# Sixteen gathered blocks instead of fourteen in a graph layer with residual and normalisation

## Chip, cores and metric

The kernel runs on one core of a Trainium2 chip. The metric is device time in microseconds (us). Before the change, three runs gave a median of 632.7 us (629.24 to 637.61). One more execution, taken with the hardware profiler, is the source of every duration below; it took 545.63 us.

## The reference

A graph has 6250 nodes with 128 features each and 100,000 edges, sorted by their destination. An edge has a source, a destination and a type (0 or 1). Each edge carries the message of its source node, made with one of two weight matrices by the edge's type; messages are summed at the destination. The node's own row goes through a third matrix, and the result is added to the input and normalised.

```python
Xs = X[src]
m_data = Xs @ W_data.T + b_data
m_ctrl = Xs @ W_control.T + b_control
msg = jnp.where((edge_types == 0)[:, None], m_data, m_ctrl)
agg = jax.ops.segment_sum(msg, dst, num_segments=X.shape[0])
out = jax.nn.relu(agg + (X @ W_self.T + b_self))
x = _layernorm(x + out)
```

## The kernel before

**Blocks.** The 6250 nodes are 49 blocks of 128 rows (`NB`). Since edges are sorted by destination, the edges of one destination block lie in one window of 18 x 128 edges (`KT` = 18). The engines are named as in the profile: PE does matmuls, ACT and DVE work on tiles and empty PE's output, POOL issues indirect DMAs, SP issues plain ones.

**Build (up to about 90 us).** For every source node and both edge types, PE computes the message row (`y`, L460 and L462). The row is kept as three bf16 parts whose sum is the fp32 value, so it has 3 x 128 = 384 columns (`D3`); `take` and `leave` (L467 to 480) split it off. All message rows stay on the chip in `m3`, as 98 source tiles (49 blocks times two types, `NT`), and are also stored to a table in memory (`store`, L482).

**Packed destination blocks.** The first 35 blocks (`NPB`, the sum of `GROUPS`) are packed, in seven groups of five.

- Ranking (`ranks`, L550): for each of 18 columns of edges, matmuls with `tri` and `rest` (32-column strips of 128 rows, output `acc`, 490 columns for five blocks: 98 tiles times 5) count how many edges of the same source tile came before; DVE reads the count with a reduction (`slot`, L563). Each step needs the one before it. 
- Packing (`fill_a`, `fill_b`, `fill_c`, L569 to 705): edges get places in 32 slots per source tile; the lists are written to memory (`packed`) and read back spread over all partitions (`spread`, L712). Edges over 32 in a slot are listed, and their rows are gathered by an indirect DMA into `mixed` (L693 to 697), one per group, on POOL's queue.
- Per block, 25 rounds (`NS`): `gather` (L745) selects rows of `m3` with up to four matmuls of 384 columns into a PSUM tile `g_ps`, 98 in all; `evict` (L757) copies that tile to SBUF, on ACT, and for blocks of the last group on ACT or DVE; `add_up` (L771) adds it into the destination rows with four more matmuls (100 in all), through a one-hot matrix `hot_d` that DVE makes.

**Gathered destination blocks.** The other 14 blocks (`NG`) take their messages from the table: for each of their 18 columns, POOL issues one indirect DMA of 128 rows of 384 values (`gather_rows`, L854) into one of `MB` = 5 message tiles; DVE makes a one-hot matrix for six columns at once (`hot_g`, L866), and PE adds the tile with four matmuls (`gathered_sums`). A gather waits until the tile `MB` gathers earlier has been read by PE.

**Ends.** Each block gets its own row by 8 matmuls (`own_of`), is summed, and waits for normalisation by group: packed ones by `PIECES` (the last group in two pieces), gathered ones by `GQ` blocks (5, 5 and 4).

**Order.** All these loops are streams of steps with assumed costs. A planner (`Order`) runs once when the program is written: at each engine it takes, among the steps that can start, the one with the earliest due time, and the instructions are issued in that order. An engine then runs its list strictly in order. `due` (L388) sets the due times: packed blocks every `BLOCK` = 13.1 us from `BUILT` = 76 us on, gathers every `PACE` = 1.75 us; the groups' packing ends `AHEAD` = 26 us before the group is begun.

```python
free = [("gm", *gathered[i - MB])] if i >= MB else [*stored, "idx"]
yield step(("msg", j, k), {"G": PACE}, *free, lag=3.0 - PACE)
```

`PACE` is thus the planned distance of gathers and their assumed time on POOL.

Of the kernel before, what the change touches and what calls it, by code (L numbers as in the profile page):

```python
# [32 lines left out]
ES = ER // RJ  # L33
EPS = 1e-05

GROUPS = (5,)*7
Q = max(GROUPS)
NPG = len(GROUPS)
NPB = sum(GROUPS)
NG = NB - NPB  # L40
STARTS = [sum(GROUPS[:i]) for i in range(NPG)]
R = 32
# [58 lines left out]
def step(name, costs, *needs, lag=0.0):  # L101
    return as_tuple(name), costs, [as_tuple(n) for n in needs], lag
# [7 lines left out]
def kernel(  # L110
# [95 lines left out]
    with ExitStack() as main:  # L206
        sums_over_windows(main, tc, x, xt, edges, w, bias, table, packed, total,
                          add_parts, finish, load_rows, norm)
# [6 lines left out]
def sums_over_windows(ctx, tc, x, xt, edges, w, bias, table, packed, total,  # L215
# [67 lines left out]
    for j in range(RJ):  # L283
# [17 lines left out]
    counted = {n: const.tile([P, P, n], BF16, name=f"count{n}")  # L301
               for n in sorted({DC, CH, *GROUPS})}
    tri = const.tile([P, P], BF16, name="tri")
# [5 lines left out]
    slot_values = [const.tile([P, (Q + 1) // 2, NT], BF16, name=f"vs{i}") for i in range(2)]  # L309
    slot_b = {n: const.tile([P, R, n], BF16, name=f"slot{n}") for n in sorted({*GROUPS})}  # L310

# [70 lines left out]

    LEAD, BUILT = 8.0, 76
    BLOCK = 13.1
    PACE = 1.75
    AHEAD, FIRST = 26.0, 20

    def due(kind, *i):  # L388
        if kind in ("p", "g") and i[0] in ("root", "rooted", "scale", "apply", "out"):
            n = i[1] + 1  # L390
            return BUILT + 10 + (BLOCK * sum(p[2] for p in PIECES[:n]) if kind == "p" else PACE * KT * GQ * n)
        if kind in ("counted", "turned", "first"):
# [21 lines left out]
        if kind in ("win", "xs", "agg", "o", "whole", "sum"):  # L414
            b = i[0]
            begun = BUILT + (BLOCK * b if b < NPB else PACE * KT * (b - NPB))
            if kind == "win":
                return due("fields", blocks[b][0]) - 8 if b < NPB else BUILT - 20
            if b >= NPB:
                return begun + {"whole": PACE * KT + 2, "sum": PACE * KT + 5}.get(kind, 0)  # L420
            return begun + {"whole": BLOCK + 0.5, "sum": BLOCK + 3}.get(kind, 0.3 * BLOCK)
# [4 lines left out]
        if kind in ("gh", "gm", "msg"):  # L426
            k = i[1] * CH if kind == "gh" else i[1]
            return BUILT + PACE * (i[0] * KT + k) + {"msg": 0, "gh": 2, "gm": 5}[kind]
        n = GROUPS[i[0]]
# [402 lines left out]
    rel_g = const.tile([P, NG, KT], BF16, name="rel_g")  # L832
    msgs, g_hots, kept = {}, {}, []
    GQ = -(-NG // -(-NG // Q))
    MB, XB = 5, 2

    def gathered_fields():
        yield step("idx", {"V": 1.8}, ("y", NB * 3 // 4), *[("win", b) for b in range(NPB, NB)])
# [10 lines left out]
    def gather_rows():  # L849
        for i, (j, k) in enumerate(gathered):  # L850
            free = [("gm", *gathered[i - MB])] if i >= MB else [*stored, "idx"]
            yield step(("msg", j, k), {"G": PACE}, *free, lag=3.0 - PACE)
            msgs[j, k] = late.tile([P, D3], BF16, name="msg", bufs=MB)
# [190 lines left out]
```

## Time and profile before

| what | value |
|---|---|
| median of three runs | 632.7 us |
| the profiled execution | 545.63 us |
| its span, first to last instruction | 543.9 us |
| mean granted clock of PE | 0.989 of full speed |
| PE busy | 504.0 us, 93% |
| DVE, ACT, POOL busy | 425.9, 422.6, 296.4 us |
| gathers | 252, first at 88.7 us, last at 520.4 us |
| DMA traffic | 79.20 MB, 146 GB/s in the mean |

A group's row gives the line, engine, operation, what it writes and reads, the count, then busy time and the mean duration of one in ns, then idle time of the engine before these instructions and what ended it. Durations of matmuls overlap, four strips of 32 columns run side by side, and so their sum is far above the busy time. L232 is a helper, `by_columns`, that issues four matmuls; the tiles tell which loop it served.

### The profile page before, as it was taken

What the parts mean: (1) busy time and instruction counts of PE and PEld (TensorE: products, weight loads), DVE (VectorE), ACT (ScalarE), POOL (GpSimd) and SP (SyncE); (2) the same over time, 40 slices, a digit from 0 to 9 for tenths busy, and PEclk for the clock granted to TensorE, in tenths of its full rate; (3) what the DMA queues carried; (4) which work ended last, traced back from release to release, by engine and by line L of the source; (5) the groups of instructions that cost most, each with busy time, mean ns of one, the idle gap of its engine ahead of it and who ended that gap; (6) DMA issues with size and microseconds to landing.
All of it is one profiled execution on the core that took longest, in us unless ns stands there. A gap on an engine that the chain in (4) does not pass through costs nothing.

```text
span 543.9 us, 26402 instructions
## 1 busy us (share of the span) xinstructions
PE 504.0 (93%) x11222; PEld 440.7 (81%) x11222; DVE 425.9 (78%) x958; ACT 422.6 (78%) x1012; POOL 296.4 (54%) x267
## 2 busy tenths in 40 slices
PE   4899978999899999999999999999999999979990
PEld 3555538799789999898998989989988898869990
DVE  4677679778887889888799788988798766867872
ACT  6745556697778888879879797798789987978782
POOL 1000004776766667767487576676677556676610
PEclk9999989999999999999999999999999999999996
DMA  3466984444454443645445445444355542646211
GB/s 110 134 178 189 285 278 136 147 142 124 138 149 154 140 128 128 174 124 156 139 137 153 134 140 169 155 147 118 114 179 169 160 140 62 194 143 189 91 46 30
DMA packets 60934, 79.20 MB, mean 146 GB/s; under 512 B 15761, under 2 KB 51372, under 8 KB 60808
## 3 DMA queue, kind: packets, MB, share of 16 engines
q1 hardware_dynamic: 47253, 48.95, 28.0%
q0 software_dynamic: 12400, 25.08, 16.9%
q10 hardware_dynamic: 1154, 3.41, 1.8%
q8 instruction: 89, 1.46, 1.1%
q14 instruction: 38, 0.30, 0.2%
HBM read 64.35 MB, written 13.05 MB: 142 GB/s over the span
## 4 chain that ended last, share of the span: by engine, by line
PE 72%; DMA 11%; DVE 9%; ACT 3%; issue 2%; SPq 1%; POOL 1%; DVEq 0%; ACTq 0%; POOLq 0%
PE agg L232 23%; PE g_ps L754 22%; PE acc L232 8%; PE small L600 7%; PE agg_g L232 7%; DMA msg<-table,idx 5%; DMA rows<-packed 5%; PE y L460 2%; DVE hot_st L546 2%; DVE slot L563 1%; ACT gs L769 1%; ACT h_p L190 1%; PE y L478 1%; DVE rows L725 1%; ACT h_g L190 1%
## 5 line engine op out<-in xcount | busy, mean ns | idle before, releaser
L769 ACT CAST gs<-g_ps 128x384 bf16<-128x384 f32 x807 | 334.3, 495 | 71.3 <-PE g_ps L754 58.2
L854 POOL DMA_INDIRECT msg<-table,idx x252 | 285.9, 1135 | 133.7 <-PE g_ps L754 64.9
L754 PE MATMUL g_ps<-m,rows 128*32 128x384 bf16 x3430 | 319.1, 331 | 0.0
L232 PE MATMUL agg<-gs,hot_d 128*32 128x384 bf16 x3360 | 298.2, 329 | 3.7 <-ACT gs L769 3.2
L754 PEld LDWEIGHTS <-rows 128*32 128x32 bf16 x3430 | 187.2, 136 | 16.8 <-issue 10.1
L232 PEld LDWEIGHTS <-hot_d 128*32 128x32 bf16 x3500 | 188.8, 137 | 11.4 <-issue 6.8
L232 PE MATMUL agg_g<-msg,hot_g 128*32 128x384 bf16 x1008 | 108.0, 329 | 7.2 <-DMA msg<-table,idx 6.8
L563 DVE TENSOR_REDUCE slot<-acc 128x5 bf16<-128x490 f32 x126 | 83.5, 663 | 36.3 <-PE acc L232 28.3
L739 DVE TENSOR_TENSOR hot_d<-count,to 128x1664 bf16<-128x1664 bf16 x70 | 74.7, 1068 | 8.1 <-PE agg L232 7.9
L600 PE MATMUL small<-hot_st,two 128*32 128x98 bf16 x1260 | 72.5, 290 | 0.0
L600 PEld LDWEIGHTS <-two 128*32 128x32 bf16 x1260 | 59.1, 117 | 3.6 <-issue 1.4
L232 PEld LDWEIGHTS <-hot_g 128*32 128x32 bf16 x1008 | 53.0, 124 | 11.0 <-issue 9.4
L232 PE MATMUL acc<-hot_st,rest 128*32 128x490 bf16 x476 | 54.4, 376 | 7.9 <-DVE slot L563 7.8
L232 PE MATMUL acc<-hot_st,tri 128*32 128x490 bf16 x504 | 60.5, 375 | 1.1 <-DVE hot_st L546 1.1
L471 ACT CAST m<-y 128x512 bf16<-128x512 f32 (+1 forms) x75 | 40.6, 580 | 26.1 <-PE y L478 18.8
L694 POOL DMA_INDIRECT mixed<-table,row_i x7 | 8.2, 1169 | 86.5 <-PE g_ps L754 80.5
L546 DVE TENSOR_TENSOR hot_st<-count,st_b 128x2940 bf16<-128x2940 bf16 x21 | 41.9, 1999 | 7.7 <-PE small L600 6.3
L725 DVE TENSOR_SCALAR rows<-rows,pid 128x3136 bf16<-128x3136 bf16 x35 | 37.2, 1062 | 6.0 <-DMA rows<-packed 6.0
L232 PEld LDWEIGHTS <-rest 128*32 128x32 bf16 x476 | 21.7, 97 | 17.8 <-issue 16.3
L460 PE MATMUL y<-w_sb,xt 128*128 128x256 f32 x98 | 31.3, 407 | 1.8 <-DMA xt<-in_xt 1.8
L153 DVE TENSOR_REDUCE whole<-agg 128x128 f32<-128x384 f32 x35 | 19.3, 552 | 12.3 <-PE agg L232 9.2
L769 DVE CAST gs<-g_ps 128x384 bf16<-128x384 f32 x33 | 18.0, 555 | 12.9 <-PE g_ps L754 12.4
(140 smaller groups left out, 426.2 us busy)
## 6 DMA issues: line engine op xcount, KB each, us to landing
rows<-packed SPq DMA_DIRECT2D x35, 784.0 KB
table<-m SPq DMA_DIRECT2D x10, 768.0 KB
msg<-table,idx POOLq DMA_INDIRECT x252
xt<-in_xt ACTq DMA_DIRECT2D x5, 512.0 KB
xt_p<-in_xt SPq DMA_DIRECT2D x35, 64.0 KB
xs_p<-in_x SPq DMA_DIRECT2D x35, 64.0 KB
out<-h_p SPq DMA_DIRECT2D x6, 320.0 KB
table<-m SPq DMA_DIRECT2D x2, 480.0 KB
```

Of the source, the lines that this page charges most:

```text
L153: nc.vector.tensor_reduce(whole, agg.rearrange("p (i c) -> p c i", i=3), axis=AX.X, op=ALU.add)
L232: T.matmul(out[c : c + 32], lhsT[:, c : c + 32], rhs, **flags)
L460: T.matmul(y[:, j, :], xts[g][:, b + j - at_part[g], :], w_sb[:, : 2 * D], start=j == 0, stop=False, skip_group_check=True)
L471: A.copy(part_of(b, n, i), ys[b][:, :n, :].rearrange("p b (t c) -> p t b c", t=2))
L546: V.tensor_tensor(hot, counted[n][:, None, 1 : NT + 1, :].to_broadcast([P, KC, NT, n]), fields[grp][2][:, c * KC : c * KC + KC, None, :].t ...
L563: V.tensor_reduce(slots[grp][:, k, :], by_q, axis=AX.X, op=ALU.max)
L600: T.matmul(vt[c0 : c0 + R, q // 2, :], two[:, k % KC, i, :, q], hot[:, k % KC, :, q], start=k == 0 and q < 2, stop=k == KT - 1, skip_group ...
L725: V.tensor_scalar(rows[b], rows[b], pid1, None, op0=ALU.is_equal)
L739: V.tensor_tensor(hot, counted[DC][:, :, :n], places[grp][:, q, None, c * DC : c * DC + n].to_broadcast([P, P, n]), op=ALU.is_equal)
L754: T.matmul(g_ps[t * R : (t + 1) * R, :D3], rows[b][:, :, s], m3[:, s, :], start=True, stop=True)
L769: (A.copy if e == "A" else V.tensor_copy)(gs[at], g_tiles.pop((b, g))[at, :D3])
L854: G.indirect_dma_start(out=msgs[j, k], out_offset=None, in_=table[:, :], in_offset=bass.IndirectOffsetOnAxis(ap=idx[:, j, k : k + 1], axis=0),
```

## The change

Two blocks move from the packed to the gathered kind: 33 packed blocks in six groups of five and one of three, and 16 gathered ones with 288 gathers instead of 252. Message tiles are six instead of five. The planned distance of gathers is 1.4 us instead of 1.75.

```diff
-GROUPS = (5,)*7
+GROUPS = (5,)*6+(3,)
...
     BLOCK = 13.1
-    PACE = 1.75
+    PACE = 1.4
     AHEAD, FIRST = 26.0, 20
...
     GQ = -(-NG // -(-NG // Q))
-    MB, XB = 5, 2
+    MB, XB = 6, 2
```

By these, other sizes follow: the last group's tiles are three blocks wide (294 columns in `acc`), its end pieces are of two blocks and one, the help of DVE in `evict` covers its three blocks, a further pair of constants for width three is made in the build stage, and the gathered blocks are normalised in four pieces of four. All due times of gathered steps come from the new `PACE`, and so the planner's order on every engine is another.

## Prediction

> **What bounds the kernel now.** I read the page's busy shares first, then its chain, then the groups, and last the waits and the timeline for the steps that the change touches.
>
> ```profile
> PE 504.0 (93%) x11222; PEld 440.7 (81%) x11222; DVE 425.9 (78%) x958; ACT 422.6 (78%) x1012; POOL 296.4 (54%) x267
> PE 72%; DMA 11%; DVE 9%; ACT 3%; issue 2%; SPq 1%; POOL 1%; DVEq 0%; ACTq 0%; POOLq 0%
> L854 POOL DMA_INDIRECT msg<-table,idx x252 | 285.9, 1135 | 133.7 <-PE g_ps L754 64.9
> L754 PE MATMUL g_ps<-m,rows 128*32 128x384 bf16 x3430 | 319.1, 331 | 0.0
> L232 PE MATMUL agg<-gs,hot_d 128*32 128x384 bf16 x3360 | 298.2, 329 | 3.7 <-ACT gs L769 3.2
> L232 PE MATMUL agg_g<-msg,hot_g 128*32 128x384 bf16 x1008 | 108.0, 329 | 7.2 <-DMA msg<-table,idx 6.8
> ```
>
> TensorE is busy 93% and holds 72% of the chain, and its groups have next to no idle time before them. POOL, which issues the gathers, is busy 54%, and its idle time ends on PE: it waits for message tiles to be read. So PE sets the pace and POOL follows. The stages confirm it (columns: stretch, length, busy time of PE, PEld, DVE, ACT, POOL, clock, DMA share, GB/s):
>
> ```profile
> 60.00:80.00 20.00, 16.43 (x198) 9.12 (x200) 13.77 (x34) 9.99 (x22) 0.00 (x0) 0.96 0.83 270
> 180.00:200.00 20.00, 20.00 (x518) 19.33 (x513) 16.09 (x29) 16.79 (x44) 13.20 (x12) 1.00 0.42 124
> 480.00:500.00 20.00, 17.44 (x414) 15.99 (x409) 14.81 (x32) 15.50 (x40) 14.43 (x13) 1.00 0.51 159
> ```
>
> The build stage has slack on PE; from about 90 us on there is hardly any, except in places such as 480 to 500. Matmul durations overlap, so I price PE by starts. The timeline of PE:
>
> ```profile
> 505.52 0.40 PE L232 MATMUL agg_g<-msg,hot_g 128*32 128x384 bf16 x4
> 505.68 0.40 PE L754 MATMUL g_ps<-m,rows 128*32 128x384 bf16 x4
> 505.84 0.40 PE L232 MATMUL agg<-gs,hot_d 128*32 128x384 bf16 x4
> ```
>
> Four matmuls of 384 columns start every 0.163 us: 0.041 us each. From the longest dense pieces of the chain, a packing matmul (L600) costs 0.042 us (24 in 1.03); for a ranking matmul of 490 columns I scale the 384-column price: 0.052 us, and 0.031 us for 294 columns.
>
> **What the Trainium skill says.** TensorE: Matmul & The Clock Gate, "Wait — 56ns, not 53.3ns?": a warm matmul of N columns starts N ÷ 2.4 GHz + about 2.5 ns after the last; 384 columns give 162 ns (estimate), and the 163 ns above agree, with four column strips running as one. The same page, "Seeing it yourself": a peak-current limit takes a die to 13/16 of the clock once three of its cores run dense matmuls. The trace does not show it (clock 0.989). GPSIMD Engine Reference, "1. Specifications": GpSimd shares its SBUF interfaces with VectorE, with contention. The trace agrees in kind: gathers take 948 ns at the median but 1135 ns in the mean, some over 2 us.
>
> **The two clocks.** The profiled execution took 545.6 us (span 543.9); the runs shown have a median of 632.7, 87 us more. About 411 us of dense PE work lies between the first gathered matmul and the end; at 13/16 it would take 411 × (1/0.8125 − 1) = 95 us more, less some stalls that it would cover. That fits 87 us. So I take it, as an estimate that no trace shows, that the timed runs had a PE clock near 0.81. This choice decides the forecast.
>
> **The change, part by part.** *Two packed blocks go.* Each has 98 selecting matmuls (L754), 100 adding ones (L775 to 779, shown as L232) and 36 packing ones: 2 × (198 × 0.041 + 36 × 0.042) = 19.3 us. The last group keeps its 140 ranking matmuls, but at 294 columns instead of 490: 140 × 0.021 = 2.9 us. *Two gathered blocks come:* 36 message tiles of four matmuls, 36 × 0.163 = 5.9 us. The own-row matmuls, 8 per block and kind, are the same for both. **Net on PE: −16.3 us** at full clock, from about 477 to 461 us of dense work over the built program's order; −20.1 us at 0.8125. It all lies after the build stage, where PE has no slack, so it counts.
>
> *ACT and DVE.* 50 evictions of 0.495 us go; two row selections (1.06), four hot_d (1.07) and the narrower ranking go from DVE; six hot_g (0.55) come. Both get lighter: nothing, as PE covers them. The help of DVE in eviction covers the last three blocks instead of five; in either order about two unhelped blocks follow the last packing, so I take 0 (−2 to +3). A third count constant and slot constant go into the build stage, where ACT is busy half the time: 0 (0 to 0.5).
>
> *The short last group* ranks 18 steps in 39 planned us instead of 65. In the program's order its steps stand 2.0 us of PE work apart; in the build stage a five-wide step, PE to DVE (0.66) and back, took 1.4 us. I take 0, at most +4.
>
> *Thirty-six more gathers, due every 1.4 us.* POOL, back to back, needs 1.135 + 0.30 us between them = 1.435. In the old order PE has 1.63 us of dense work per gather and met stalls of 6.8 us on messages; in the new one the first and last gathered matmul stand at 61 and 442 of 461 us: 381/288 = 1.33 us. With 1.036 for PE's other stalls that is 1.37 us at full clock, less than POOL can give, and 1.69 at 0.8125, as roomy as before. At the slow clock I take +3 (0 to +8), as the old order had less than 7 to lose there and the sixth tile gives one gather more ahead. Behind a late message stands all of PE, as its order is fixed; then ACT, which has nothing to evict.
>
> *SP:* two window loads move ahead of those of later groups, two row broadcasts go, four loads per packed block become four per gathered: covered, SP has a due time of tens of us there. *End:* the gathered blocks now finish some 19 us of PE work before the packed ones. Before, their apply (1.65 us on ACT) and scales stood in front of the last block's own:
>
> ```profile
> 531.38 0.54 DVE whole L153
> 533.04 1.65 ACT h_g L190 x4
> 535.97 0.49 ACT h_p L190
> ```
>
> Without them the last apply comes about 1.6 us sooner. A fourth normalising piece in mid-run is covered.
>
> Sum for the timed runs: 632.7 − 20.1 + 3 − 1.6 = 614. Spread of the small terms: −24 to −6, so 608 to 627. In the profiled execution, at full clock, −16.3 − 1.6 would give 527 if nothing else bound; the next part says why I expect more there.
>
> **Rivals.** *1. POOL becomes the bound (slower).* Its place is the gather queue; its price is 1.435 us. POOL begins at 87.5 us: 288 × 1.435 + 7 spilled gathers × 1.47 + 6 us of waits for their lists = 430, so the last gather starts near 516; the chain shows 3.6 to 5.6 us from start to use:
>
> ```profile
> 138.94 4.18 DMA msg<-table,idx
> 206.01 4.70 DMA msg<-table,idx
> ```
>
> Its matmuls come at 520, then 19 us × 1.04 of packed work, 540, and the end of 11 us: 551 span, 552.7 us, +1.3%. If PE and POOL also wait by turns (now POOL idles 58 us beyond its 0.30 per gather; a sixth of that would be 10 us), +3%. On the timed scale 641 to 652; I take 645. It decides where PE's 1.37 us ÷ clock falls under about 1.49, that is above a clock of 0.92. For it: the profiled clock, 0.989, and the stall at 480 to 500, where gathers stand as densely as the change puts them everywhere. Against it: 632.7. *In the profile after, if its clock is near 1, I expect this case: 540 to 555 us.*
>
> *2. The gain is lost in small waits* (messages landing late, the short ranking chain, ACT at 25 evictions × 0.42 us per block, close to PE's pace in the last blocks). Half of 20 us lost: 623 to 633, no change.
>
> *3. The clean gain:* gathers never late, ACT's relief counts too: 605.
>
> *4. It doesn't do what it says:* the count of matched edges fails and the slow fallback runs. Nothing in the group sizes bears on the windows; 1 in 100.
>
> **How the numbers follow.** The forecast (608 to 620), 0.38; clean gain, 0.08; small waits (620 to 633), 0.25; POOL bound, 0.28, of which about 0.20 over +2% (645.4); fallback 0.01. About 2% is what a measurement can tell from no change. So faster 0.46, within 0.33, slower 0.21. The range leaves out the fastest tenth and the worst tenth: 605 to 646. The likeliest is 614; the forecast's own range is 608 to 620.
>
> **What would show it.** PE records fall from 11222 to some 10880 and L754 from 3430 to 3234 (−196); msg gathers are 288. Right at a slow clock: PE waits on msg under 10 us. POOL bound: PE's waits for messages rise to 20 us and more in many places, POOL's idle time falls to its 0.30 per gather, and gathers come 1.44 to 1.5 us apart to beyond 510 us. The forecast is wrong if the timed runs had the full PE clock, and their 87 us came from something that gathers share.

## The result, and the profile after

The change made the kernel slower: 671.9 us (median of 4 runs, 670.4 to 672.6) against 633.9 us before, a ratio of 1.061 (95% interval 1.057 to 1.066). The profiled execution of the change is one of these runs: 672.6 us, span 670.8 us. Where runs of one kernel on one chip lie more than 1.5% above its fastest, ratios leave them out.

These runs were slower for both kernels than the profile shown of before and all experiments below, where the same kernel before took 549 to 552 us and the change 561 (1.016 on one chip, 1.019 on another). The experiments ran on four chips; that the result's runs came from a fifth, slower one is likely, but its number is not on record. So two things have to be explained, a loss of some 2% that shows on the other chips, and a larger one in the runs of the result.

The page of the change in those runs, busy times, the granted clock and the groups that answer to those of before:

```profile
PE 561.9 (84%) x10890; PEld 428.0 (64%) x10890; DVE 412.6 (62%) x955; ACT 415.7 (62%) x975; POOL 325.4 (49%) x303
PEclk9999897999899999989999999999998999999996
PE 73%; issue 8%; DVE 6%; ACT 6%; DMA 4%; SPq 1%; POOL 0%; ACTq 0%; another core or an unknown queue 0%; DVEq 0%; POOLq 0%
L854 POOL DMA_INDIRECT msg<-table,idx x288 | 316.2, 1098 | 213.9 <-PE agg_g L232 90.0
L754 PE MATMUL g_ps<-m,rows 128*32 128x384 bf16 x3234 | 326.7, 338 | 24.5 <-issue 13.7
```

The work is what the change says: 3234 selecting matmuls, 288 gathers, 332 matmul records fewer. Yet every engine is busy for a smaller share of the span than before, POOL too: its idle time before gathers rose to 213.9 us. The granted clock is full but for some slices with a piece at half clock. The waits of the same kernel (engine, line, what ended the idle time: us in total, times, longest; "issue" where the engine waited for nothing that the profile shows), and below them those of the profile before:

```profile
ACT gs L769 <- PE g_ps L754: 125.6, 161, 2.6
PEld L232 <- issue: 114.2, 230, 4.0
PEld L754 <- issue: 50.0, 105, 2.0
PE agg_g L232 <- DMA msg<-table,idx: 1.0, 1, 1.0
```

```profile
ACT gs L769 <- PE g_ps L754: 58.2, 100, 2.9
PEld L232 <- issue: 35.5, 69, 1.9
PEld L754 <- issue: 10.1, 46, 0.2
```

PE waits 1.0 us for messages, less than before (6.8). POOL is not the bound here. PE's weight loads stand idle 164 us for nothing that the profile names, against 46 before, and ACT waits for PE twice as long as before. The timeline shows what such a stop looks like (lines of ACT, POOL and SP left out):

```profile
311.15 0.49 PE L754 MATMUL g_ps<-m,rows 128*32 128x384 bf16 x4
311.27 0.15 PEld L232 LDWEIGHTS <-tri 128*32 128x32 bf16 x4
311.31 0.52 PE L232 MATMUL acc<-hot_st,tri 128*32 128x490 bf16 x3
311.99 0.37 PE L232 MATMUL acc<-hot_st,tri 128*32 128x490 bf16 x1 [0.16 <-issue]
312.00 0.13 PEld L754 LDWEIGHTS <-rows 128*32 128x32 bf16 x1 [0.58 <-issue]
```

Four matmuls belong to one ranking step and wait for the same thing. Their weights are loaded by 311.42 us. Three start, the fourth comes about 0.5 us late, and the next weight load stands too. No semaphore lies between them. Counted over all groups of four after 95 us (selecting, adding, gathered and ranking matmuls, each at its place in its group), this trace has more than 50 such gaps of 0.4 to 0.8 us; the same program on other chips (e5, e12, e18) and the kernel before (e11) have none.

These are the clearest of many. After 95 us, the starts of two successive matmuls lie more than 0.2 us apart 366 times in this trace, 195 us in sum, and 132 times, 72 us, in that of the same program in e12. The difference of 123 us covers the 111 us between the two spans. The stops also come in trains: 276 starts come over 0.3 us after the one before, and of the 275 intervals between these, 67 are 0.65 to 0.80 us long, whatever tiles the matmuls work on; in e12 it is 1 of 68. POOL is not slower here (a gather takes 0.946 us at the median, 0.947 in e12), nor are the packets of the larger queue that the profile calls "instruction" (1.07 us in the mean, 1.10 in e12). As far as these figures go, it is PE's own stream of instructions that stops. What stops it isn't shown; that instructions reach PE too late is one guess, and no run tests it.

### The profile page after: what moved, and what is told of

It reads as the page before. It is cut to its first block, busy times and chain, and to the rows that moved or that the text cites. A ratio compares the mean times of both kernels' runs of the same rounds, so it can differ in the third digit from the quotient of the medians.

```text
span 670.8 us, 25712 instructions
## 1 busy us (share of the span) xinstructions
PE 561.9 (84%) x10890; PEld 428.0 (64%) x10890; DVE 412.6 (62%) x955; ACT 415.7 (62%) x975; POOL 325.4 (49%) x303
## 4 chain that ended last, share of the span: by engine, by line
PE 73%; issue 8%; DVE 6%; ACT 6%; DMA 4%; SPq 1%; POOL 0%; ACTq 0%; another core or an unknown queue 0%; DVEq 0%; POOLq 0%
PE agg L232 25%; PE g_ps L754 24%; PE agg_g L232 9%; PE acc L232 7%; PE small L600 6%; ACT gs L769 4%; PE y L460 2%; DVE slot L563 1%; DMA table<-m 1%; ACT h_p L190 1%; DVE hot_st L546 1%; DMA rows<-packed 1%; PE y L478 1%; DVE whole L153 0%; DVE hot_d L739 0%
## 5 line engine op out<-in xcount | busy, mean ns | idle before, releaser
L854 POOL DMA_INDIRECT msg<-table,idx x288 | 316.2, 1098 | 213.9 <-PE agg_g L232 90.0
L754 PE MATMUL g_ps<-m,rows 128*32 128x384 bf16 x3234 | 326.7, 338 | 24.5 <-issue 13.7
L232 PE MATMUL agg<-gs,hot_d 128*32 128x384 bf16 x3168 | 300.2, 341 | 32.7 <-issue 15.9
L232 PEld LDWEIGHTS <-hot_d 128*32 128x32 bf16 x3300 | 193.9, 137 | 82.3 <-issue 71.8
L563 DVE TENSOR_REDUCE slot<-acc 128x5 bf16<-128x490 f32 (+1 forms) x126 | 80.1, 636 | 91.4 <-PE acc L232 43.8
L232 PE MATMUL agg_g<-msg,hot_g 128*32 128x384 bf16 x1152 | 124.1, 333 | 5.1 <-issue 3.9
L739 DVE TENSOR_TENSOR hot_d<-count,to 128x1664 bf16<-128x1664 bf16 x66 | 70.5, 1071 | 21.8 <-PE g_ps L754 14.3
L232 PEld LDWEIGHTS <-hot_g 128*32 128x32 bf16 x1152 | 59.8, 125 | 11.3 <-issue 9.3
L232 PE MATMUL acc<-hot_st,tri 128*32 128x490 bf16 (+1 forms) x504 | 60.6, 369 | 3.7 <-issue 2.2
L232 PE MATMUL acc<-hot_st,rest 128*32 128x490 bf16 (+1 forms) x476 | 53.8, 370 | 11.6 <-DVE slot L563 9.5
L600 PEld LDWEIGHTS <-two 128*32 128x32 bf16 x1188 | 52.5, 116 | 13.2 <-issue 11.4
L546 DVE TENSOR_TENSOR hot_st<-count,st_b 128x2940 bf16<-128x2940 bf16 (+1 forms) x21 | 39.9, 1905 | 19.2 <-PE small L600 13.0
L725 DVE TENSOR_SCALAR rows<-rows,pid 128x3136 bf16<-128x3136 bf16 x33 | 34.2, 1035 | 5.4 <-DMA rows<-packed 5.3
L232 PEld LDWEIGHTS <-rest 128*32 128x32 bf16 x476 | 21.4, 99 | 24.0 <-issue 23.2
L232 PEld LDWEIGHTS <-tri 128*32 128x32 bf16 x504 | 21.9, 99 | 8.3 <-issue 7.7
```

The source lines that it names most:

```text
L232: T.matmul(out[c : c + 32], lhsT[:, c : c + 32], rhs, **flags)
L546: V.tensor_tensor(hot, counted[n][:, None, 1 : NT + 1, :].to_broadcast([P, KC, NT, n]), fields[grp][2][:, c * KC : c * KC + KC, None, :].t ...
L563: V.tensor_reduce(slots[grp][:, k, :], by_q, axis=AX.X, op=ALU.max)
L600: T.matmul(vt[c0 : c0 + R, q // 2, :], two[:, k % KC, i, :, q], hot[:, k % KC, :, q], start=k == 0 and q < 2, stop=k == KT - 1, skip_group ...
L725: V.tensor_scalar(rows[b], rows[b], pid1, None, op0=ALU.is_equal)
L739: V.tensor_tensor(hot, counted[DC][:, :, :n], places[grp][:, q, None, c * DC : c * DC + n].to_broadcast([P, P, n]), op=ALU.is_equal)
```

## The same program where before takes 551 us

The change was run three more times beside the kernel before (e5, e12, e18). Here its page reads differently. Busy times, POOL by slices, and the group of the gathers, of e12:

```profile
PE 495.1 (89%) x10890; PEld 428.4 (77%) x10890; DVE 411.0 (73%) x955; ACT 409.8 (73%) x975; POOL 334.7 (60%) x303
POOL 1000003777778787777787787877787777777100
L854 POOL DMA_INDIRECT msg<-table,idx x288 | 325.3, 1130 | 94.4 <-PE g_ps L754 44.0
```

POOL's idle time before gathers fell from 133.7 us for 252 of them to 94.4 for 288: 0.33 us each, hardly more than the 0.30 that it always has. And POOL ends two slices before the span does. Waits of e12, then of the kernel before on the same chip (e11):

```profile
PEld L232 <- issue: 63.8, 89, 4.6
PE agg_g L232 <- DMA msg<-table,idx: 27.8, 24, 3.7
```

```profile
PEld L232 <- issue: 39.3, 71, 2.0
PE agg_g L232 <- DMA msg<-table,idx: 6.8, 8, 1.5
```

PE waits four times as long for messages; the weight loads behind such a matmul then stand too, which the profile puts down to "issue" (of the 63.8 us, 36.2 stand before the loads of `hot_g`, which belong to these matmuls, against 9.3 in e11; so much of the two rows is one stop seen from two sides, and they are not added). The longest one, 3.7 us, in PE's timeline (lines between left out) and in POOL's, both of e12:

```profile
431.70 0.39 PE L232 MATMUL agg_g<-msg,hot_g 128*32 128x384 bf16 x4
436.01 0.38 PE L232 MATMUL agg_g<-msg,hot_g 128*32 128x384 bf16 x4 [3.69 <-DMA msg<-table,idx]
```

```profile
427.01 0.95 POOL L854 DMA_INDIRECT msg<-table,idx  x1 [0.30 <-PE small L678]
428.26 1.25 POOL L854 DMA_INDIRECT msg<-table,idx  x1 [0.30 <-PE g_ps L754]
429.82 1.24 POOL L694 DMA_INDIRECT mixed<-table,row_i  x1 [0.31 <-issue]
431.36 0.95 POOL L854 DMA_INDIRECT msg<-table,idx  x1 [0.30 <-PE g_ps L754]
432.62 0.95 POOL L854 DMA_INDIRECT msg<-table,idx  x1 [0.30 <-PE g_ps L754]
```

POOL issues one gather after another with 0.30 us between them and has the group's spilled rows (`mixed`) to gather as well, and still the message comes too late. That it is POOL's own time that is missing, and not room in the tiles, is what e7 tests.

## Experiments

Theory P: POOL can't issue the gathers as fast as PE's list asks for them, and PE, whose order is fixed, waits. Rivals are named with the runs. Every ratio is to runs of before on the same chip.

**e1, e11, e13, e15, e17: the kernel before, unchanged,** to learn whether PE's stops belong to it as well.

> The kernel before, unchanged, profiled once more. Theory A (PE stalls that no wait explains belong to both kernels in their timed runs, and the profile of before shown first happened to have none): 625 to 640 us in the profile too, with PE idle put down to issue of 60 to 120 us instead of 35. Theory B (the denser gathers of the change hold PE up): about 546 us in the profile, and few such stalls.

> The kernel before, once more, to have its trace from the chip of this call. If this chip is like the one of the result (before at 634 us): PE idle put down to issue of 60 to 120 us. If it is like that of e1 to e8: 546 to 555 us and about 49 us of such idle time.

> The kernel before, unchanged, in a further call. If it takes about 551 us again, nothing new: PE idle put down to issue about 49 us. If it takes about 634 us, as in the runs of the result: 60 to 120 us of such idle time, and gaps of 0.4 to 0.8 us between matmuls of one group of four, as in the trace of the change.

> The kernel before, unchanged. If it takes about 634 us, as in the runs of the result: 60 to 120 us of PE idle put down to issue, and gaps of 0.4 to 0.8 us inside groups of four matmuls. If about 551: as in e1.

> The kernel before, unchanged. About 634 us, as in the runs of the result: 60 to 120 us of PE idle put down to issue, and gaps of 0.4 to 0.8 us inside groups of four matmuls. About 551: as in e1.

They took 551.7, 551.2, 551.1, 550.6 and 550.3 us on four chips, each with 35 to 40 us of idle weight loads at L232, as in the profile of before. None of them has the 634 us of the result, so no trace of before with that time exists. Theory A falls on these chips; theory B's 546 us is near. The profile shown of before (545.6 us) was no odd execution: these chips give about its time.

**e2: only the block split.**

```diff
-GROUPS = (5,)*7
+GROUPS = (5,)*6+(3,)
```

> Only the 16 gathered blocks; five message tiles and the planned distance of 1.75 us as before. Theory A (stalls follow the program's PE stream, whatever the gathers' pace): between the kernels, 610 to 670 us. Theory B (the pace of gathers costs the time): close to or under before, 610 to 640 us. Theory C (the short last group): as slow as the whole change, 660 to 680 us.

589.5 us, 1.071 (1.065 to 1.076): worse than the whole change, so the split can't be separated from the planned distance. With 1.75 us between them 288 gathers need 504 us. The windows at its end (columns as before):

```profile
500.00:520.00 20.00, 17.31 (x412) 15.69 (x404) 13.57 (x40) 14.30 (x36) 11.93 (x13) 0.99 0.29 75
520.00:540.00 20.00, 8.49 (x80) 2.88 (x81) 2.81 (x8) 0.08 (x1) 15.13 (x17) 0.50 0.32 86
540.00:560.00 20.00, 8.44 (x77) 2.57 (x77) 2.80 (x7) 0.00 (x0) 15.13 (x17) 0.50 0.30 80
```

The packed blocks are done at 516 us, some 20 us sooner than in e11 (536 us), as two of them are gone. Then ACT has nothing to do and PE does 80 matmuls in 20 us, at half clock, one message at a time. The times expected were written for the chip of the result; as a ratio, theory C's "as slow as the whole change" is the nearest, but not for C's reason: what stands at the end are gathers, not the short group.

**e3: only the planned distance.**

```diff
-    PACE = 1.75
+    PACE = 1.4
```

> Only the planned distance of gathers, 1.4 us instead of 1.75, with 14 gathered blocks and five tiles. Theory B: most of the loss, 650 to 680 us. Theory C (the short group, or the block count): as before, 625 to 640 us.

574.4 us, 1.044 (1.038 to 1.050). Without any block moved, the distance alone costs more than the whole change does on such chips: theory B. Waits and the windows at its end:

```profile
PE agg_g L232 <- DMA msg<-table,idx: 25.0, 32, 2.3
```

```profile
460.00:480.00 20.00, 19.42 (x468) 17.89 (x464) 12.21 (x22) 17.16 (x42) 11.43 (x11) 1.00 0.48 138
500.00:520.00 20.00, 20.00 (x435) 16.02 (x428) 13.71 (x37) 18.58 (x48) 0.87 (x1) 1.00 0.39 133
520.00:540.00 20.00, 18.74 (x428) 16.36 (x427) 16.92 (x31) 16.67 (x41) 0.00 (x0) 1.00 0.33 107
```

The price is paid twice. While gathers run, PE waits for them, 25 us; after 480 us POOL has none left, and the packed work stands alone, at some 430 matmuls in 20 us, where e11 has 468 in the mean from 100 to 520 us, with ACT busy 17 to 19 us of 20. From 500 us on ACT does 48 instructions in 20 us, 0.42 us each; at that rate the 25 evictions of a block take 10.4 us of ACT, for 8 us of PE (estimates). The second price is larger here than in the whole change, where 36 more gathers fill the end.

**e4: only the sixth tile** (`MB, XB = 6, 2` in before).

> Only six message tiles instead of five. Theory B and C: as before, 625 to 640 us. If where the tiles lie in memory matters (every later buffer of the same pool moves by 768 bytes), it may differ by several per cent in either direction.

549.4 us, 0.996 (0.993 to 0.998): no cost, a gain of 0.4%, as theories B and C expected.

**e5, e12, e18: the whole change.**

> The whole change, unchanged, measured once more, to have it beside the kernels above on a chip where before takes about 551 us. Theory P (POOL cannot issue the gathers fast enough, about 1.45 us each, and PE waits for messages): 555 to 570 us, PE waiting 20 to 50 us for messages, POOL idle close to 0.30 us a gather. Theory S (PE halts without any wait, in runs of whatever chip, because of the new order): about 585 us, idle put down to issue above 100 us, hardly a wait for messages.

> The whole change once more, beside the trace of before on the same chip. On a chip where before takes about 634 us, as in the result: 665 to 675 us, hardly a wait for messages, PE halts without a wait of over 150 us. On one where it takes about 551: 553 to 566 us and 20 to 40 us of waits for messages.

> The whole change, with five rounds. Where before takes about 551 us: 1.01 to 1.025 of it, 20 to 40 us of waits for messages. Where it takes about 634 us: 1.05 to 1.07, hardly a wait for messages.

e5: 553.6 and 559.9 us beside 551.1, too few for an interval; e12: 561.5 beside 551.4, 1.016 (1.007 to 1.024), on the same chip as e5; e18: 561.1 beside 549.0, 1.019 (1.013 to 1.024), on another. The loss is small, but both intervals lie above 1. Waits for messages 28.0, 27.8 and 29.3 us. Theory P holds, theory S (PE halts of its own) doesn't, on these chips.

**e7: nine tiles with the change** (`MB, XB = 9, 2`), to tell POOL's rate from the depth of the buffer.

> The change with nine message tiles instead of six. If too few tiles hold the gathers back, POOL's idle time and PE's waits for messages fall and it gains 2% or more, to 545 to 555 us. If POOL's own time per gather is the limit, within 1% of the change.

554.5 us, 1.005 (1.003 to 1.008): 1% better than e12, between the two expectations, so the time alone doesn't decide. The waits do: PE's for messages stay at 26.7 us, while POOL's longest before a gather is now 0.3 us, 87.8 us for all 288. POOL runs without a pause and PE waits nevertheless: the rate is the limit.

**e6, e14: a distance that POOL can keep.**

```diff
-    PACE = 1.4
+    PACE = 1.5
```

> The change with a planned distance of 1.5 us instead of 1.4: about what POOL gave in the runs above (1.43 to 1.53 us a gather). Theory P, with the order as the way in which it hurts (gathers planned sooner than they come): 1 to 2% faster than the change, 545 to 560 us. Theory P with the rate alone as the limit: within 1% of the change.

> The change with a planned distance of 1.5 us, again. Theory Q: 0.97 to 0.985 of before where before takes 551 us. Where before takes 634 us, the halts of PE that no wait explains decide instead: 1.02 to 1.06 of before, if they come with the changed list of PE whatever the gathers' distance.

540.5 us, 0.978 (0.971 to 0.985), and on another chip 541.2, 0.984 (0.980 to 0.988). With the distance changed and nothing else, the same split of blocks is 1.6 to 2.2% faster than before. Beside the change it gains 3.7%, more than either theory expected. Waits and windows of e6:

```profile
PE agg_g L232 <- DMA msg<-table,idx: 15.7, 16, 3.8
```

```profile
500.00:520.00 20.00, 20.00 (x479) 17.76 (x474) 15.97 (x41) 16.32 (x41) 14.64 (x16) 1.00 0.37 97
520.00:540.00 20.00, 6.10 (x136) 4.63 (x124) 8.21 (x30) 6.03 (x16) 4.18 (x5) 0.72 0.20 54
```

Gathers and packed blocks end together: the last gathered matmul starts at 527.1 us, the last of a packed block at 524.2. In e12 these are 526.6 and 545.4. So the gathers are through at the same time in both, as POOL's rate sets it; the 18 us between the spans (541.4 and 559.3 us) lie behind that point, 14.3 us against 32.7. What PE loses in e12 while it waits for messages is packed work that it then does alone at the end.

**e9, e10: what of the distance hurts.** `PACE` is both the assumed cost on POOL and the distance of the due times. e9 has 1.5 as cost and 1.4 in the due times, e10 the reverse:

```diff
-            yield step(("msg", j, k), {"G": PACE}, *free, lag=3.0 - PACE)
+            yield step(("msg", j, k), {"G": 1.5}, *free, lag=3.0 - 1.5)
```

> The change, with the planner charging 1.5 us of POOL for a gather while the due times keep the distance of 1.4 us. Theory Q (what hurts is that gathers are over early and packed work stands alone at the end: 18.7 us of PE work behind the last gathered matmul, here 8.6): in between, 545 to 556 us. Theory R (what hurts is a PE list that reckons with messages sooner than they land): as good as e6, 538 to 545 us.

> The change, with due times 1.5 us apart while the planner still charges 1.4 us of POOL for a gather. Theory Q (only 2.6 us of PE work is left behind the last gathered matmul, as in e6): as good as e6, 538 to 545 us. Theory R: close to the change, 553 to 563 us.

e9: 560.4 us, 1.016 (1.009 to 1.022), as slow as the change; e10: 548.5, 0.987 (0.975 to 0.999). Both theories missed both: Q expected e9 in between and e10 as good as e6, R expected e9 good and e10 slow. It is the due times that matter, and the assumed cost hardly does. PE's waits follow how densely its list asks for messages, counted in the built program as PE's own work from the first gathered matmul to the last, per gather, priced by starts (estimates):

| run | PE work per gather, us | left behind the last, us | PE's waits for messages, us | ratio |
|---|---|---|---|---|
| e11 (before) | 1.63 | 5.6 | 6.8 | 1 |
| e8 (15 blocks, 1.6) | 1.50 | 4.9 | 8.8 | 0.983 |
| e6 (change, 1.5) | 1.38 | 2.6 | 15.7 | 0.978 |
| e10 (due 1.5) | 1.38 | 2.6 | 18.8 | 0.987 |
| e9 (cost 1.5) | 1.36 | 8.6 | 24.6 | 1.016 |
| e12 (change) | 1.33 | 18.8 | 27.8 | 1.016 |
| e3 (14 blocks, 1.4) | 1.37 | 71.7 | 25.0 | 1.044 |

The times do not follow that density alone. e3 has 71.7 us of packed work left. e9 is as slow as e12 with less left, as its last gathered matmul starts 8 us later than that of e6, at 535.0 us; its gathers took 1.143 us in the mean, those of e6 1.115, which makes 8 us over 288.

**e8: fifteen gathered blocks.** `GROUPS = (5,)*6+(4,)`, `PACE = 1.6`, six tiles.

> Fifteen gathered blocks, 34 packed ones (the last group four wide), six tiles, planned distance 1.6 us. PE has then about 1.54 us of its own work per gather, just over POOL's 1.45. Theory P: at or under before, 540 to 552 us. If any move of blocks costs by itself (a narrower last group): above before, 555 to 565 us.

543.5 us, 0.983 (0.975 to 0.991), as theory P expected: a narrower last group costs nothing that shows, and one block moved gains, where the gathers keep up.

**e16: distance 1.5 and nine tiles,** the fastest version tried.

> The change with a planned distance of 1.5 us and nine message tiles. The tiles gained about 1% at 1.4 us (e7 beside e12). If they let POOL keep going where PE is held up by other things: 530 to 538 us where before takes 551. If with 1.5 us POOL's own time is all that is left: 538 to 545 us.

535.4 us, 0.971 (0.965 to 0.978), PE's waits for messages down to 9.8 us: the first of the two expectations.

## Why the prediction was wrong

The step that failed is **the two clocks**. I took the 87 us between the profile of before and its timed runs for a PE clock near 0.81, and said that this choice decides the forecast. The trace of the change, from a run of 672.6 us, shows a granted clock of 0.972 in the mean: full clock, with half clock in six pieces of 3 to 7 us and at the very end. The other three runs have 0.965 to 0.973. So the peak-current limit of the Trainium skill (TensorE: Matmul & The Clock Gate, "Seeing it yourself") was not at work in them. The same section says that one or two busy cores never trip it, and this kernel runs on one; the prediction passed over that. What the trace of the change shows in place of a slow clock is stops of PE at nearly full clock: 195 us between starts over 0.2 us apart, against 72 us in e12. That a sum fitted 87 us was a coincidence as far as the record goes; the clock of the runs of before at 634 us is not on it. A gap between profile and timed runs that no trace shows was made the ground of a forecast.

The prediction named this way to be wrong ("if the timed runs had the full PE clock"), but a PE that is slow at full clock was not among its cases: for a clock near 1 it expected 540 to 555 us in the profile after, and that profile took 672.6. Its sign for a slow clock, under 10 us of waits for messages, came true with 1.0 us and so can't tell a slow clock from any other slowness of PE.

- *The net of −16.3 us on PE:* right as work (10890 records; 3234 and 288 as listed), but at the result it did not become time. In its trace PE has 9225 matmul records in the 520 us from 100 to 620 us, 17.7 per us, and in e12 9358 in the 420 us from 100 to 520, 22.3 per us. The stops that no wait explains took more than the 16 us; whether the kernel before has fewer of them there is not known.
- *+3 us for gathers at a slow PE:* on the result's chip PE waited 1.0 us for messages, so the term held; POOL followed there, as I said it would if PE was slow. It was the reason for PE's slowness, and so its size, that was wrong.
- *Rival 1, POOL becomes the bound:* right in mechanism where before takes 551 us, near the 545.6 us of the profile before. Gather starts: predicted 1.44 to 1.5 us apart, measured 1.486 in e12; last gather: predicted 516 us, measured 519.7; waits for messages: predicted 20 us and more, measured 27.8; span: predicted 551, measured 559.3. Of the 8.3 us, 3.7 come from a later last gather, and that from a later begin: the first gather of e12 starts at 93.3 us, that of the profile before at 89.0 (the 88.7 us given ahead of the prediction are the end of the instruction in front of it). I gave the added constants 0.5 us at most, but they are not shown to be the reason: e3, which has none, begins at 91.9. Another 2.9 us lie between the last gather and its matmul (6.9 us, where I had 4), and 1.7 behind that: 32.7 us to the end, where I had 31. Of these, 19 us are the packed work, as priced.
- *Its place in the chances:* the profiled clock, the stall at 480 to 500 us and the count of 1.37 us asked against 1.435 given all spoke for it; only 632.7 us against it. I gave it 0.28.
- *The last apply comes 1.6 us sooner:* right, but no gain. From the last block's sum to the end of its apply e12 needs 3.5 us, e11 5.1; what follows it, the last store among it, takes back 2.4.
- *The short last group and ACT's help:* PE's wait for ranking results is 9.4 us in e12 and 10.4 in e11: no cost, as taken; e8 agrees.

**What stays open.** Why the change loses 6.1% where before takes 634 us, instead of 1.6 to 1.9%. The trace of the change there says that PE stops for 0.4 to 0.8 us in the middle of groups that wait for nothing, and that messages are in time. Whether the kernel before has such stops there, fewer or shorter ones, would need its trace from such a chip; there is none. Nor was the version with 1.5 us tried there, so its gain is shown for chips of the other kind only.

## What to carry to other kernels

When work moves to another engine, price that engine at its mean distance from start to start under load, here 1.13 us of gather and 0.30 between, and ask whether the fixed order of the consumer demands more: 1.33 us of PE work per gather against 1.435 given was visible ahead. The due times that a planner gives a stream must not be closer than its engine can keep: with due times 1.5 us apart most of the gain came though the assumed cost stayed at 1.4 (e10), and with the cost alone at 1.5 none did (e9). Two streams that fill each other's gaps should end together, as each alone runs into its own limit. Where the profile and the timed runs differ by 16%, find out why before a forecast is built on one of them.

## What the runs showed of the hardware

In the lone end of e2, with DVE busy 2.8 us in 20, nearly every gather takes POOL 0.94 to 0.95 us (two of the 39 from 520 us on took 1.05 and 1.27):

```profile
533.43 0.95 POOL L854 DMA_INDIRECT msg<-table,idx  x1 [0.30 <-issue]
534.68 0.95 POOL L854 DMA_INDIRECT msg<-table,idx  x1 [0.30 <-issue]
535.93 0.94 POOL L854 DMA_INDIRECT msg<-table,idx  x1 [0.30 <-issue]
```

That is one every 1.25 us, while under load the mean is 1.13 + 0.33 = 1.46 in e12. The Trainium skill (GPSIMD Engine Reference, "1. Specifications") says that GpSimd shares its SBUF interfaces with VectorE, and that DVE instructions with two SBUF inputs or in a 2-port mode contend for them. The traces agree and give the size. Two gathers of e12, each with the DVE instruction that it met:

```profile
302.97 0.66 DVE L563 TENSOR_REDUCE slot<-acc 128x5 bf16<-128x490 f32 x1
303.20 0.95 POOL L854 DMA_INDIRECT msg<-table,idx  x1 [0.30 <-issue]
```

```profile
350.07 2.00 DVE L546 TENSOR_TENSOR hot_st<-count,st_b 128x2940 bf16<-128x2940 bf16 x1 [1.30 <-PE small L600]
350.12 2.77 POOL L854 DMA_INDIRECT msg<-table,idx  x1 [0.31 <-PE small L600]
```

Counted over the traces of all twenty runs, by what DVE did in the first 0.94 us of a gather:

| DVE in that time | gathers | a gather took, us |
|---|---|---|
| nothing | 465 | 0.94 to 0.96 |
| only the ranking reduction, out of PSUM (L563) | 216 | 0.94 to 0.95 |
| only `hot_st`, two SBUF inputs (L546) | 253 | 1.77 in the mean, up to 2.77 |
| only `hot_d`, two SBUF inputs (L739) | 184 | 1.27 in the mean |
| only the row selection, one SBUF tensor (L725) | 114 | 1.33 in the mean |

So it is not a busy DVE that slows a gather, but some of its instructions; in the mean this makes 0.18 us, or 19%, per gather of 128 rows in e12. It is read from what overlaps; no run changed DVE's instructions. Not expected, and not explained, are the stops of PE inside a group of four, 0.4 to 0.8 us, more than 50 of them, in the one trace of the result.
